# A two-layer Perceiver kernel on one Trainium2 core: its RWKV stage issued in three pieces a block

## The chip, the core and the metric

The kernel runs on one core of one Trainium2 chip. The core has five engines that run at the same time, each through an instruction list of its own: PE (TensorE, matrix products and transposes; its weight loads are listed as PEld), DVE (VectorE, elementwise work, scans and reductions), ACT (ScalarE, functions such as exp), POOL (GpSimd, elementwise work) and SP (SyncE, which here issues most DMAs). An instruction that needs another engine's result waits on a semaphore, and everything behind it on its own engine waits with it. So the order in which an engine's list is written decides as much as the amount of work.

The metric is the device time of one execution in microseconds (us). The profile is one more execution, recorded by the hardware profiler.

## What is computed

The input x has 64 sequences of 32 tokens of width 256, 2048 tokens; the context has 64 sequences of 257 rows. Two layers of three residual parts each run one after the other:

```python
x = x + _L0_xattn_ref(_layernorm(x), ctx_1024, ctx_1024, mask, ...)   # cross attention
x = x + _L0_attn_ref(_layernorm(x), ...)                              # RWKV
x = x + _L0_ffn_ref(_layernorm(x), ...)                               # 8 experts, top 2
x = x + _L1_xattn_ref(_layernorm(x), ctx_1024, ...)                   # quantized cross attention
x = x + _L1_attn_ref(_layernorm(x), ...)                              # state-space recurrence
x = x + _L1_ffn_ref(_layernorm(x), ...)                               # experts, top 1
```

The part that the change touches is the RWKV, whose two halves are a time mix (a recurrence over the 32 tokens of a sequence) and a channel mix:

```python
h = layernorm(x, ln1_g, ln1_b)
hh = time_shift(h)                     # the token before, 0 for the first
xk = h * tm_k + hh * (1 - tm_k)        # likewise xv, xr
k, v = xk @ Wk.T, xv @ Wv.T
sr = sigmoid(xr @ Wr.T)
x = x + (sr * wkv(time_decay, time_first, k, v)) @ Wo.T     # wkv: the recurrence
h = layernorm(x, ln2_g, ln2_b)
hh = time_shift(h)
xk = h * cm_k + hh * (1 - cm_k)        # likewise xr
kk = square(relu(xk @ Wck))
return x + sigmoid(xr @ Wcr.T) * (kk @ Wcv)
```

All of it works within a sequence, so blocks of whole sequences are independent of each other.

## The kernel before

The tokens are cut into 4 blocks of 512, and a block into 4 tiles of 128 tokens (4 sequences each). The residual stream x stays in on-chip memory for the whole kernel, one buffer a block (`k.x[b]`); every stage adds to it in place. All matrix products are in f32.

There are six stages, each a function that sets up its weights and returns what runs one block:

- `_stage0`, the first cross attention (here "stage 0"): `s0(b)` is a head (norm, transposes, query) and four tiles, 16 in all. A tile computes scores (L259), a softmax, the weighted sum (L292), the output product and its addition to x (L300). It also quantizes the context for the fourth stage: GpSimd multiplies the loaded context cT by its scales (L248), VectorE rounds, and a DMA stores the result (cq). `steps()` closes this.
- `_stage1`, the RWKV: `s1(b)`, L487 to L548, described below.
- `_stage2`, the first expert layer: `s2(b)` normalizes, computes the router's logits (L585), a softmax and the choice of two (L595 to L616) on VectorE, transposes the gates (gT, L619), then for each tile adds the gated bias (beps, L626) and the products of all 8 experts (weps, L631), which VectorE scales and adds to x (L633).
- `_stage3`, the second cross attention: `s3(lo, hi)` runs some of its 32 units (eight a block): scores L881, softmax, transposes (pt, L907), weighted sum (L915) and, with `last`, the closing norms and products of the block; the last of them is named vl_ps.
- `_stage4`, the state-space recurrence: `ahead(b)`, `gates(b)`, `recur(b)`; a block's recurrence is 32 groups of a multiply g on GpSimd (L1096), exponentials on ScalarE (L1100), scans on VectorE (L1101), a multiply hc (L1102) and a sum on GpSimd (L1107).
- `_stage5`, the second expert layer: up (L1250) and acc (L1258) products.

**One block of the RWKV.** VectorE takes the moments of the four tiles and an inverse root is made in twelve small GpSimd steps (`_rsqrt`, L90 to L93). `norm_to` (L435) writes the normalized rows hn (L446), PE transposes them (tps, L124), and ScalarE copies them into `hT`, a padded buffer in which channels lie on the partitions and tokens along the row. `shift_mix` (L408) takes the difference of `hT` and its shifted self and makes the mixes from it. Then `recur(c, ...)` (L449) runs once for each half c of the 256 channels: projections k, v and r (L432), a scan for the running maximum (L460), exponentials, two more scans (bb L474, aa L475), a reciprocal (L481), and the product with the gate sr (L484 on GpSimd, rw L485 on VectorE). GpSimd makes e2bv (L466) and v (L478) between. After both halves the output projection (wo, L507) is added to the normalized rows xn, which GpSimd made at L502, and to x. A second norm, transposes and shift mix follow, then the gate product (cr, L520) with a sigmoid, and the channel mix: eight groups of up products (ck, L528), Relu (L530) on ScalarE, square (kk, L531) on GpSimd and four products into the sum (cv, L540), with `up` two groups ahead; at the end VectorE multiplies by the gate (sg, L545) and GpSimd adds to x (L546).

**Buffers.** The recurrence's temporaries come from the pool `u1` with 9 buffers; each half needs six of them (v, sr, pp, e1, aa, bb). The padded buffers kp, e1b, e2b, e2bv exist once for each half; `hT` exists once and serves both norms of a block. hn, xn and sg share three buffers (tag "rows"), the mixes three others (tag "mix").

**Order.** The program is written stage by stage in `layers` (L1284 on). The framework that the kernel is written in schedules each engine's list when the kernel is built, ahead of the run: instructions whose inputs are expected ready are taken by the place at which they were emitted. So the order in `layers` is the priority, and an instruction that was emitted earlier goes first where both are ready. The lists are fixed after that. In the order of before, `s1(0)` is emitted behind `s0(1)`, `s1(1)` behind `s0(2)`; `s1(2)` and `s1(3)` are emitted at the end of their group, behind `s0(3)`, `s2(0)` and the first eight units `s3(0, 8)`, so that they fill what these leave free. The pools of the RWKV lie on the left side of the memory and are released when `s1(3)` is done; the state-space stage's buffers come there.

Of the kernel before, what the change touches and what calls it, by code (L numbers as in the profile page):

```python
# [8 lines left out]
F32 = mybir.dt.float32  # L9
# [6 lines left out]
P = 128  # L16
NB, T, S, D = 64, 32, 257, 256
NTOK = NB * T
NT = NTOK // P
NBLK = 4  # L20
# [336 lines left out]
def _stage1(k, pool):  # L357
# [4 lines left out]
    nc, i = k.nc, k.i  # L362
    w, u, wk, sm1 = pool("w1", 1), pool("u1", 9), pool("wk1", 1), pool("small1", 2)
    pa, pb = pool("psa1", 2, space=bass.MemoryType.PSUM), pool("psb1", 2, space=bass.MemoryType.PSUM)
# [13 lines left out]
    def padded(name, fill, shape=(16, T + 1)):  # L378
        t = w.tile([P, *shape], F32, name=name, tag=name)
        nc.gpsimd.memset(t, fill)  # L380
        return t

    wt, kp, e1b, e2b, e2bv = [], [], [], [], []
    for c in range(2):
        wt.append(padded(f"wt{c}", BIG))
        nc.vector.tensor_copy(wt[c][:, :, 1:], wdec[:, c : c + 1].unsqueeze(2).to_broadcast([P, 16, T]))
        kp.append(padded(f"kp{c}", BIG))
        e1b.append(padded(f"e1b{c}", 0.0))
        e2b.append(padded(f"e2b{c}", 0.0))
        e2bv.append(padded(f"e2bv{c}", 0.0))  # L390
    hT = padded("hT", 0.0, (2, 16, T + 1))

# [12 lines left out]
    def rows(name):  # L405
        return wk.tile([P, 4, D], F32, name=name, tag="rows", bufs=3)

    def shift_mix(names):  # L408


        def mix(name):
            return wk.tile([P, 2, 16, T], F32, name=name, tag="mix", bufs=3)

# [20 lines left out]

    def norm_to(xs, mean, scale, g, b):  # L435

# [49 lines left out]

    def block(b):  # L487
        x = k.x[b]
# [5 lines left out]
        _rsqrt(k, r8, [(mv[:, :, 1], 1.0, LN_EPS), (mv[:, :, 1], 1.0 + LN_EPS, LN_EPS * LN_EPS)], "1", sm1)  # L494
        norm_to(x, mv[:, :, 0:1], r8[:, 4:8], "L0_attn_ln1_g", "L0_attn_ln1_b")
        xk, xv, xr = shift_mix(["L0_attn_tm_k", "L0_attn_tm_v", "L0_attn_tm_r"])
        rw = wk.tile([P, 2, BT], F32, name="rw", tag="rw", bufs=1)
        for c in range(2):
            recur(c, xk, xv, xr, rw)
        xn = rows("xn")  # L500
        for j in range(4):
# [9 lines left out]

        mv2, rstd2 = _stats(k, [xn[:, j, :] for j in range(4)], "1b", sm1)
        norm_to(xn, mv2[:, :, 0:1], rstd2, "L0_attn_ln2_g", "L0_attn_ln2_b")
        xk, xr = shift_mix(["L0_attn_cm_k", "L0_attn_cm_r"])
        sg = rows("sg")
        for j in range(0, 4, 2):
            p = pa.tile([P, 2, D], F32, name="cr", tag="a")
            for f in range(2):
                for c in range(2):
                    nc.tensor.matmul(p[:, f, :], xr[:, c, (j + f) * P : (j + f + 1) * P], wT["cr"][:, c, :], start=c == 0, stop=c == 1)  # L520
            nc.scalar.activation(sg[:, j : j + 2, :], p, AF.Sigmoid)

        cvs = [pb.tile([P, 2, D], F32, name="cv", tag="b") for _ in range(2)]
# [23 lines left out]

    return block  # L548

# [729 lines left out]
def layers(k, out):  # L1279
# [13 lines left out]
    with left0:  # L1293
        s1 = _stage1(k, opened(left0, "left"))
        with ExitStack() as es:
            s0, steps = _stage0(k, opened(es, "right"))
            s0(0)
            for b in range(1, NBLK):
                s0(b)
                if b < NBLK - 1:  # L1300
                    s1(b - 1)
            steps()
# [7 lines left out]
        s3(0, 8, first=True, last=True)  # L1310
        s1(NBLK - 2)
        s1(NBLK - 1)
    with right, right3, left:
        pool = opened(left, "left")
# [130 lines left out]
```

## Time and profile before

| | us |
|---|---|
| median of three runs | 2054.96 |
| the runs | 2054.96, 2054.93, 2056.96 |
| the profiled execution, its own time | 2053.01 |
| its span, from the first to the last instruction | 2051.2 |

| engine | busy us | share of the span | instructions |
|---|---|---|---|
| PE | 1618.9 | 79% | 6323 |
| PE weight loads | 819.6 | 40% | 6323 |
| DVE | 1367.5 | 67% | 2475 |
| ACT | 983.5 | 48% | 2142 |
| POOL | 1062.7 | 52% | 1189 |

| mark in the span | us |
|---|---|
| channel mix of block 0 on PE | 219 to 247 |
| recurrence of block 1 (first scan to last rw) | 275.8 to 312.8 |
| channel mix of block 1 on PE | 349 to 377 |
| last sum of stage 0 | 396.6 |
| recurrence of block 2 | 401.1 to 438.6 |
| first matmul of the first expert layer (beps, L626) | 440.5 |
| first scores of the second attention (L881) | 484.0 |
| end of that attention's first block (vl_ps) | 690.9 |
| RWKV of block 3 ends (its last x, L546) | 705.5 |
| first scan of the state-space stage (L1101) | 778.1 |
| end | 2051.2 |

How to read what follows. A profile line of the timeline begins with the start in us and the length, then the engine, the source line, the operation, its output and inputs by the program's names, tile shapes (rows by columns for PE, partitions by elements otherwise), and how many equal instructions in a row it stands for. Where a bracket ends it, it holds the idle time of the engine just before and what ended it: `[11.47 <-PE cv L540]` is 11.47 us without work until PE's cv of L540 was done. Lines of the kernel are named L531 and so on. No engine is full over the span: the shares are means over stages with different limits, and the granted clock of PE, 0.831 of full speed on average, differs from stage to stage.

### The profile page before, as it was taken

Reading aid. Unit: us, or ns where it says so; the run is one execution under the profiler, and the core shown is the slowest. Engines: PE = TensorE matmul, PEld = TensorE weight load, DVE = VectorE, ACT = ScalarE, POOL = GpSimd, SP = SyncE. Lnnn points to the kernel's source line nnn. Section 1 sums busy time; section 2 is a strip of 40 time slices with the busy share of each in tenths; the row PEclk is TensorE's granted clock in tenths of the full one; section 3 lists DMA queues with packets and bytes.
Section 4 is the critical chain, followed back from the end, with each engine's and each line's share of the span. In section 5 each row is a group of like instructions: output and inputs, shape, how many; then the busy total and the mean of one; then the engine's idle time right before and its main releaser. Section 6 shows DMA issues by size and latency. Waiting matters only on the chain. (4 is left out here: it accounts for less than half of the span.)

```text
span 2051.2 us, 20219 instructions
## 1 busy us (share of the span) xinstructions
PE 1618.9 (79%) x6323; PEld 819.6 (40%) x6323; DVE 1367.5 (67%) x2475; ACT 983.5 (48%) x2142; POOL 1062.7 (52%) x1189
## 2 busy tenths in 40 slices
PE   4775967759979888765788969878879677688898
PEld 3332524425645543433443434444434233233343
DVE  4488487575475459989965887864778785886200
ACT  2454343313455254444427656637567454564332
POOL 5344656423142306776641776771477766998000
PEclk9677867879989998556689779988789889899999
DMA  6754324210000211222101222302123211442121
GB/s 223 234 188 135 113 72 145 64 41 21 21 21 2 61 28 42 58 56 61 42 32 48 73 66 89 92 21 69 52 62 89 54 52 58 107 118 63 51 82 41
DMA packets 88379, 151.26 MB, mean 74 GB/s; under 512 B 7740, under 2 KB 52300, under 8 KB 86224
## 3 DMA queue, kind: packets, MB, share of 16 engines
q1 hardware_dynamic: 85428, 148.75, 24.1%
q10 hardware_dynamic: 2844, 1.22, 0.2%
q8 instruction: 50, 0.82, 0.2%
q14 instruction: 57, 0.47, 0.1%
HBM read 139.03 MB, written 10.92 MB: 73 GB/s over the span
## 5 line engine op out<-in xcount | busy, mean ns | idle before, releaser
L1096 POOL TENSOR_TENSOR g<-dtx,bc 128x1024 f32<-128x1024 f32 x128 | 301.5, 2359 | 155.8 <-DVE h L1101 79.6
L1101 DVE TENSOR_TENSOR_SCAN h<-h,g 128x512 f32<-128x512 f32 x256 | 306.7, 1218 | 55.2 <-ACT h L1100 47.3
L1107 POOL TENSOR_TENSOR xc<-xc,hc 128x1024 f32<-128x1024 f32 x128 | 302.7, 2368 | 32.0 <-DVE hc L1102 22.8
L1250 PE MATMUL up<-xT,w 128*128 128x512 f32 x512 | 286.4, 675 | 34.5 <-ACT hid L1252 32.7
L1258 PE MATMUL acc<-hid,w 128*128 128x512 f32 x512 | 269.1, 647 | 21.1 <-ACT hid L1254 21.1
L1100 ACT ACTIVATE h<-dt,A 128x512 f32<-128x512 f32 x256 | 172.3, 691 | 155.5 <-DVE hc L1102 155.1
L892 ACT ACTIVATE p<-sc,nm 128x256 f32<-128x256 f32 x256 | 117.7, 471 | 135.8 <-DVE nm L888 121.9
L881 PE MATMUL sc<-kT,qm 32*128 32x256 f32 x512 | 147.3, 496 | 31.9 <-DVE od L921 21.9
L1102 DVE TENSOR_TENSOR hc<-h,bc 128x512 f32<-128x512 f32 x256 | 169.0, 677 | 1.6
L1250 PEld LDWEIGHTS up<-xT,w 128*128 128x128 f32 x512 | 98.2, 209 | 158.6 <-issue 84.0
L631 PE MATMUL weps<-we,xT 128*128 128x512 f32 x256 | 149.4, 710 | 14.1 <-DVE x L627 7.7
L1258 PEld LDWEIGHTS acc<-hid,w 128*128 128x128 f32 x512 | 100.1, 206 | 140.6 <-issue 100.9
L1252 ACT ACTIVATE hid<-up,chan 128x512 f32<-128x512 f32 x128 | 87.2, 681 | 133.4 <-PE up L1250 133.4
L90 POOL TENSOR_TENSOR rs_t<-rs_r 128x4 f32<-128x4 f32 (+4 forms) x168 | 37.3, 225 | 190.4 <-DVE rs_r L88 178.9
L881 PEld LDWEIGHTS sc<-kT,qm 32*128 32x128 f32 x512 | 86.2, 230 | 84.4 <-DVE od L921 32.9
L907 PE MATMUL pt_ps<-ident,p 128*128 128x128 f32 x512 | 94.3, 317 | 23.7 <-ACT p L892 16.4
L886 DVE TENSOR_REDUCE nm<-sc 128x2 f32<-128x512 f32 x128 | 86.2, 684 | 39.0 <-PE sc L881 38.3
L909 ACT COPY pt<-pt_ps 128x512 f32<-128x512 f32 x128 | 74.2, 586 | 58.1 <-PE pt_ps L907 57.8
L907 PEld LDWEIGHTS pt_ps<-ident,p 128*128 128x128 f32 x512 | 65.5, 159 | 79.3 <-ACT p L892 36.9
L1272 DVE SCALAR_TENSOR_TENSOR last<-rT,gt,x 128x256 f32<-128x256 f32 x16 | 7.6, 478 | 125.4 <-PE rT L1271 125.4
L531 POOL TENSOR_TENSOR kk<-kk 128x512 f32<-128x512 f32 x32 | 34.1, 1072 | 110.1 <-ACT kk L530 107.2
L915 PE MATMUL oT_ps<-pt,v 128*32 128x128 f32 x1024 | 74.5, 313 | 18.2 <-ACT pt L909 18.1
(404 smaller groups left out, 3182.5 us busy)
## 6 DMA issues: line engine op xcount, KB each, us to landing
bc<-rows SPq DMA_DIRECT2D x64, 512.0 KB
w<-in_L_ffn_w_dram SPq DMA_DIRECT2D x64, 512.0 KB
cT<-in_ctxT_dram SPq DMA_DIRECT2D x16, 1028.0 KB
cq<-cq SPq DMA_DIRECT2D x32, 514.0 KB
cn<-in_ctx_dram SPq DMA_DIRECT2D x64, 256.0 KB
scb<-scales SPq DMA_DIRECT2D x16, 514.0 KB
kb<-steps SPq DMA_DIRECT2D x16, 514.0 KB
x<-in_x_dram SPq DMA_DIRECT2D x4, 512.0 KB
```

The source lines that it names most:

```text
L631: nc.tensor.matmul(ps, xT[:, c, r], we[:, c, e : e + 2, :], start=c == 0, stop=c == 1)
L881: nc.tensor.matmul(sc[h][:, f, :], qm[r, e + f].rearrange("p l n g -> p (l n g)"), kTs[e][r, f, :], start=True, stop=True,)
L892: nc.scalar.activation(w_[:, f, h - h0, :], sc[h][:, f, :], AF.Exp, bias=nm[:, e + f, h : h + 1], accum_out=sm[:, e + f, h : h + 1],)
L907: nc.tensor.transpose(pt_ps[:, h, m, :], ws[e, hp][:, f, h, m * P : (m + 1) * P], k.ident)
L1096: nc.gpsimd.tensor_tensor(g, dtx[:, c2 : c2 + 2], bc[:, 0:1, :].to_broadcast([P, 2, BT]), ALU.mult)
L1100: nc.scalar.activation(h, dt, AF.Exp, scale=A[:, c2 + c, n : n + 1])
L1101: nc.vector.tensor_tensor_scan(h, h, g[:, c, :], 0.0, ALU.mult, ALU.add)
L1102: nc.vector.tensor_tensor(hc[:, c, :], h, bc[:, 1, :], ALU.mult)
L1107: nc.gpsimd.tensor_tensor(y[:, c2 : c2 + 2], y[:, c2 : c2 + 2], hc, ALU.add)
L1250: nc.tensor.matmul(u, w1[e][:, c, q * P : (q + 1) * P], xT[:, c, :], start=c == 0, stop=c == 1)
L1252: nc.scalar.activation(hid[e][:, q, :], u, AF.Identity, bias=b1)
L1258: nc.tensor.matmul(acc[o], w2[e][:, q, o * P : (o + 1) * P], hid[e][:, q, :], start=n == H, stop=n == E * H + H - 1)
```

## The change

The RWKV of a block is cut into three pieces that can be emitted apart. `time_mix(b)` goes up to the recurrence and returns its moments and rw; `between(b)` has the output projection, the second norm, its shift mix and the gate product with its sigmoid, and returns the mixed rows xk and the gate sg; `channel_mix(b)` has the eight groups of ck, Relu, square and cv, and the addition to x. The arithmetic is the same.

A new `s1(b)` emits `time_mix(b)`, then `channel_mix(b - 1)`, then `between(b)`. It is called behind each of `s0(1)`, `s0(2)` and `s0(3)`, for blocks 0, 1 and 2. So block 2 is now emitted ahead of `steps()`, `s2(0)` and the first eight units of the second attention. What was emitted behind these as blocks 2 and 3 is now block 3 (with the channel mix of block 2 in it) and the channel mix of block 3.

A channel mix now lives beside the next time mix, so the buffers change: there are two padded `hT` of which one serves the first norms and one the second; hn, xn, sg and the mixes share six buffers under one tag in place of two tags with three each; the pool `u1` has 8 buffers in place of 9; and the two halves share one e2bv buffer.

```diff
-    w, u, wk, sm1 = pool("w1", 1), pool("u1", 9), pool("wk1", 1), pool("small1", 2)
+    w, u, wk, sm1 = pool("w1", 1), pool("u1", 8), pool("wk1", 1), pool("small1", 2)
...
-        e2bv.append(padded(f"e2bv{c}", 0.0))
-    hT = padded("hT", 0.0, (2, 16, T + 1))
+        e2bv.append(e2bv[0] if c else padded("e2bv", 0.0))
+
+    hTs = [padded(f"hT{n}", 0.0, (2, 16, T + 1)) for n in range(2)]
...
-        return wk.tile([P, 4, D], F32, name=name, tag="rows", bufs=3)
-
-    def shift_mix(names):
+        return wk.tile([P, 4, D], F32, name=name, tag="rows", bufs=6)
+
+    def shift_mix(hT, names):
...
-            return wk.tile([P, 2, 16, T], F32, name=name, tag="mix", bufs=3)
+            return wk.tile([P, 2, 16, T], F32, name=name, tag="rows", bufs=6)
...
-    def norm_to(xs, mean, scale, g, b):
+    def norm_to(hT, xs, mean, scale, g, b):
...
-    def block(b):
+    def time_mix(b):
...
-        norm_to(x, mv[:, :, 0:1], r8[:, 4:8], "L0_attn_ln1_g", "L0_attn_ln1_b")
-        xk, xv, xr = shift_mix(["L0_attn_tm_k", "L0_attn_tm_v", "L0_attn_tm_r"])
+        norm_to(hTs[0], x, mv[:, :, 0:1], r8[:, 4:8], "L0_attn_ln1_g", "L0_attn_ln1_b")
+        xk, xv, xr = shift_mix(hTs[0], ["L0_attn_tm_k", "L0_attn_tm_v", "L0_attn_tm_r"])
         rw = wk.tile([P, 2, BT], F32, name="rw", tag="rw", bufs=1)
         for c in range(2):
             recur(c, xk, xv, xr, rw)
+        return mv, r8, rw
+
+    def between(b, mv, r8, rw):
+
+        x = k.x[b]
+        xs = [x[:, j, :] for j in range(4)]
         xn = rows("xn")
...
-        norm_to(xn, mv2[:, :, 0:1], rstd2, "L0_attn_ln2_g", "L0_attn_ln2_b")
-        xk, xr = shift_mix(["L0_attn_cm_k", "L0_attn_cm_r"])
+        norm_to(hTs[1], xn, mv2[:, :, 0:1], rstd2, "L0_attn_ln2_g", "L0_attn_ln2_b")
+        xk, xr = shift_mix(hTs[1], ["L0_attn_cm_k", "L0_attn_cm_r"])
...
             nc.scalar.activation(sg[:, j : j + 2, :], p, AF.Sigmoid)
+        return xk, sg
+
+    def channel_mix(b, xk, sg):
+        x = k.x[b]
...
-    return block
+    return time_mix, between, channel_mix
...
-        s1 = _stage1(k, opened(left0, "left"))
+        time_mix, between, channel_mix = _stage1(k, opened(left0, "left"))
         with ExitStack() as es:
             s0, steps = _stage0(k, opened(es, "right"))
+
+            c = {}
+
+            def s1(b):
+                t = time_mix(b)
+                if b:
+                    channel_mix(b - 1, *c[b - 1])
+                c[b] = between(b, *t)
+
             s0(0)
             for b in range(1, NBLK):
                 s0(b)
-                if b < NBLK - 1:
-                    s1(b - 1)
+                s1(b - 1)
             steps()
...
         s2(0)
         s3(0, 8, first=True, last=True)
-        s1(NBLK - 2)
         s1(NBLK - 1)
+        channel_mix(NBLK - 1, *c[NBLK - 1])
```

## The prediction

> **What bounds the kernel now.** I read the chain that ended last first. It runs back from the end only to 1568 us and is made of the state-space recurrence and the last expert layer, so the RWKV stage isn't on the part that is shown; what the stage decides is when that later work starts. The built order of the changed program agrees with the old one from the second half of the first state-space recurrence on (after its 16th of 128 multiplies g, GpSimd's counts of earlier work are equal in both), so I carry any shift there to the end unchanged. The question is when the first scan of L1101 runs; it is at 778.1 us now. I then cut the stretch before it at the events that the change moves: busy time of each engine by window (columns: window, length, busy us and instructions of PE, weight loads, DVE, ACT, POOL, then granted clock, DMA share, GB/s).
>
> ```profile
> 219.00:247.00 28.00, 27.72 (x98) 18.03 (x97) 8.62 (x13) 8.75 (x21) 18.11 (x14) 1.00 0.30 98
> 247.00:349.00 102.00, 66.48 (x312) 36.33 (x311) 84.54 (x127) 45.14 (x127) 57.65 (x60) 0.70 0.35 114
> 349.00:377.00 28.00, 28.00 (x99) 18.23 (x97) 2.51 (x3) 5.02 (x10) 11.94 (x17) 1.00 0.06 20
> ...
> 397.00:440.00 43.00, 17.02 (x56) 8.90 (x54) 39.23 (x86) 14.24 (x21) 18.84 (x38) 0.67 0.31 94
> 440.00:484.00 44.00, 41.20 (x126) 19.50 (x126) 27.70 (x84) 3.58 (x9) 8.57 (x30) 0.94 0.00 0
> 484.00:550.00 66.00, 65.89 (x341) 42.82 (x340) 28.43 (x74) 33.06 (x100) 17.50 (x20) 0.92 0.10 33
> 550.00:600.00 50.00, 42.65 (x217) 22.70 (x216) 39.30 (x71) 29.80 (x73) 15.11 (x18) 0.92 0.00 1
> 600.00:650.00 50.00, 41.84 (x189) 25.25 (x189) 30.64 (x85) 20.89 (x57) 14.16 (x41) 0.80 0.07 22
> 650.00:691.00 41.00, 41.00 (x263) 24.37 (x263) 14.35 (x37) 20.07 (x55) 10.29 (x20) 1.00 0.18 54
> ```
>
> 219 to 247 and 349 to 377 are the channel mixes of blocks 0 and 1: PE is full and DVE nearly empty. Between them, and from 397 to 440, DVE is full (84.5 of 102, 39.2 of 43) and PE starves. From 484 to 691 PE is the bound: 191.4 us busy of 207. The timelines of DVE and PE show the handovers:
>
> ```profile
> 223.63 1.08 DVE L446 TENSOR_SCALAR hn<-x,mv,r 128x256 f32<-128x256 f32 x3
> 246.22 0.69 DVE L545 TENSOR_TENSOR sg<-cv,sg 128x512 f32<-128x512 f32 x1 [11.47 <-PE cv L540]
> 250.81 0.66 PE L124 MATMUL tps<-ident,hn 128*128 128x128 f32 x4
> 275.77 1.25 DVE L460 TENSOR_TENSOR_SCAN pp<-wt,kp 128x528 f32<-128x528 f32 x1
> 296.83 2.07 PE L507 MATMUL wo<-w_L_attn_WoT,rw 128*128 128x256 f32 x4 [9.57 <-DVE rw L485]
> 312.12 0.69 DVE L485 TENSOR_TENSOR rw<-aa,sr 128x512 f32<-128x512 f32 x1 [1.07 <-POOL sr L484]
> 326.00 5.54 DVE L446 TENSOR_SCALAR hn<-xn,mv,rstd 128x256 f32<-128x256 f32 x4 [2.03 <-POOL rstd L93]
> 343.02 5.45 PE L520 MATMUL cr<-w_L_attn_WcrT,d 128*128 128x256 f32 x16
> 376.55 0.69 DVE L545 TENSOR_TENSOR sg<-cv,sg 128x512 f32<-128x512 f32 x1 [21.10 <-PE cv L540]
> 396.22 0.42 DVE L300 TENSOR_TENSOR x<-o_ps,x 128x256 f32<-128x256 f32 x1 [0.66 <-PE o_ps L298]
> 436.77 1.02 PE L619 MATMUL gT_ps<-ident,pr 128*8 128x128 f32 x4 [12.27 <-DVE pr L616]
> ```
>
> Block 1's normalized rows are ready at 224.7, but their transposes stand behind block 0's channel mix on PE and run at 250.8. Its recurrence takes 275.8 to 312.8, 37 us; block 2's took 401.1 to 438.6, the same. 396.6 is the end of stage 0.
>
> **The change, part by part.** No engine gets work or loses it, and no DMA is issued by the moved pieces; what moves is the order. On SP the loads of stage 0 and the weights of the later stages keep their number, and the stage-3 loads come after the last cq store as before.
>
> 1. Block 1's transposes go in front of block 0's channel mix: 250.8 to 224.7, 26 us earlier. The recurrence then starts at 275.8 - 26 = 250.
>
> 2. The channel mix of block 0 (28 us of PE) lies beside that recurrence. The order on GpSimd chains the two: two squares (L531, 1.04 us) and then the two matrix groups of 1.72 us stand behind the recurrence's last sr multiply (L484). Hence 250 + 37 + 2.1 + 3.4 = 292.5; the output projection, now in one piece, about 4.5 (16 passes between 0.22 and 0.38 us), ends at 297, against 313.56 + 3.96 = 317.5.
>
> 3. From there to the end of cr takes 31 us now (317.5 to 348.5); I keep it: 328. Behind it stand attention tiles 14 and 15 (two matrix chains of some 5 and 8 us by the rows at 336 to 343) and tile 16, which took 19.4 us from its scores at 377.2 to its sum at 396.6 with no channel mix in it. Stage 0 ends at 328 + 5 + 8 + 16 to 20 = 357 to 361; I take 357, 39 us earlier. Of the 39, 28 are the second channel mix, which is now emitted behind the end of stage 0 and must be paid there.
>
> 4. Block 2's recurrence starts with tile 16, about 346, and ends at 383 by the 37 us. Squares and groups as in step 2, with a reciprocal root of twelve GpSimd steps of 0.28 between them: 5.5 + 3.4, then 4.5 for the output projection: 396. Then cr: block 2's took 19 us from its last projection (471) to its start (490); 19 and 4 more: 419. Only behind cr do the expert router's logits (L585) stand now; they were at 414 to 416 before. 2 us for them, then 13: twelve DVE steps of the softmax (4.5 us by their rows) with block 3's shift mix (5.6) and an exponential between, and 1.6 for gT. The first expert matmul (L626) comes at 435, against 440.5. So most of the 39 us is spent here, on the channel mix and cr.
>
> 5. From L626 to the first scores L881 is 43.5 us now, PE 41 of 44 busy; block 3's projections come in (nine of twelve, 0.86 each, four of them in the way): 47. First scores at 482, against 484.0.
>
> 6. From the first scores to the end of the first attention (690.9) PE is the bound. It has done ahead of it 16 passes of cr, the transposes and nine projections, 13 us; but the new order puts in front of the end the last 12 products of block 3's channel mix (5.3) and 16 expert products (13.8), which stood behind it. Work 191.4 - 13 + 19 = 197. The idle 15.5 us of 550 to 650 (block 3's recurrence and its cr, waiting) get channel mix 2 and 3 as cover; I leave 6. The clock there was 0.80 and 0.92 where PE had gaps; full clock would shrink 84.5 us by some 11, I take 5. 482 + 197 + 6 - 5 = 680, 11 us earlier.
>
> 7. Behind it, the tail to the first scan was 690.9 to 778.1. The expert products that delayed the transposes of the next layer (715.9 to 724.4) and two products sg are gone from its way: 5 us, bounded by 0 and 8.5. The smaller pools (u 8 instead of 9, one e2bv) cost nothing: in every block the second half's scan already comes after the first half's reciprocal (286.3, 289.6), when slots are free, and e2bv's second write follows the first half's scan of it; the 37 us hide it, and without that cover it is one wait of about 2 us a block.
>
> Sum: 11 + 5 = 16 us. The profiled execution took 2053.0 us (span 2051.2), so 2037; the runs' median is 2 us higher, so 2054.96 - 16 = 2039; I say 2038.
>
> **A rule against the row.** The four hn of 326.00 took 5.54 us, those of 198.09 took 1.38; beside the slow ones GpSimd's cT multiply runs (325.92, 4.51 us). The Trainium skill, "SBUF — State Buffer", section "Who interferes with whom", says that VectorE and GpSimd lock a port pair against each other for a whole instruction. By that rule this change is dangerous, since it lays 16 squares beside two recurrences; an estimate from the rows is 16 x 1.04 = 17 us, and the gain would be gone. By the rows, the recurrence's 37 us hold such a collision already (rw at 291.79 took 4.98), so I add nothing.
>
> **Rivals.**
> A, the forecast, 0.50: 2038, own range 2026 to 2050.
> B, 0.16: the recurrences get faster when no attention operations stand between. Their DVE operations sum to 13 us a half by the rows (three scans 1.25, one reciprocal 3.34, eleven others 0.4 to 0.75), 26 a block against 37; with 28, two blocks give 18, and the other 6 us of the clock and 2 of the tail make 26: 2012. Against it: four recurrences in four surroundings took 37 to 46.
> C, 0.14: all is spent in front of the logits and in the tail: steps 6 and 7 give 3: about 2052.
> D, slower, 0.20: stage 0 doesn't end earlier. DVE is the bound there: between 219 and 397 it is busy 112 us, and steps 1 to 4 add some 8 in less time; collisions with GpSimd, whose cT multiply also holds back sr, stretch it. If the end stays at 396, step 4's 78 us, 47, 203 and the tail follow: 724 at the end of the first attention, 33 later, less 5: 2083. It decides from a stage 0 that ends after some 373.
> That the change doesn't take place is excluded: the built order shows it.
>
> **How the numbers follow.** A run can tell about 0.2%, 4 us, from none. Faster: A, B and a little of nothing else, 0.66. Same: 0.10 of C. Slower: D and the rest of C, 0.24. The range 2010 to 2062 cuts B's and D's outer parts, together 0.2.
>
> **What would show it.** In the changed profile: the first transposes hn of block 1 near 225 (step 1), PE waiting for GpSimd's kk within the channel mix (2), the last L300 near 357 (3), the first L626 near 435 (4), the first L881 near 482 (5), the eighth unit's last vl_ps near 680 (6), the first scan L1101 near 762 (7). Later rows must be shifted as a whole; if the distance from the first scan to the end changes by over 5 us, the assumption of equal later work is wrong. A stage 0 that ends after 373, or an L626 after 455, makes the prediction wrong.

## The result and the profile after

The changed kernel takes 2071.07 us (median of 8 runs, 2058.23 to 2079.91); the kernel before took 2053.82 us in the same comparison (8 runs, 2049.33 to 2058.81). The ratio is 1.0088, 95% interval 1.0070 to 1.0105: the change makes the kernel slower, by 17 us between the medians, where 16 us of gain were forecast.

The profiled execution took 2078.3 us (span 2076.5), 7 us above the median; a second profile of the same kernel (2078.9) shows the same marks within 3 us, and within 1.5 us from the end of stage 0 on. The steps below are measured in the first of the two, so they add up to 25 us in the span, of which the medians show 17. Line numbers behind the RWKV's first lines have moved: hn is L447, projections L433, scan L461, wo L514, cr L527, ck L539, square L542, cv L551, first scores L892, gT L630, beps L637, weps L642.

The engines' busy times first, from the page:

```profile
PE 1629.4 (78%) x6323; PEld 823.8 (40%) x6323; DVE 1386.5 (67%) x2475; ACT 982.7 (47%) x2141; POOL 1072.0 (52%) x1189
```

The instruction counts are those of before (ScalarE's but for one); VectorE is busy 19 us longer (1367.5 before), PE 10.5 and GpSimd 9.3. Whether that is the loss is a question for the experiments.

The windows of the changed kernel, cut at the same events as before (window, length, busy us and instructions of PE, weight loads, DVE, ACT, POOL, granted clock, DMA share, GB/s):

```profile
223.00:255.00 32.00, 27.85 (x134) 14.21 (x133) 28.70 (x30) 21.64 (x58) 20.17 (x10) 0.96 0.63 199
255.00:297.00 42.00, 33.50 (x111) 22.11 (x111) 24.82 (x32) 11.54 (x26) 21.90 (x26) 0.92 0.04 13
297.00:327.00 30.00, 20.14 (x103) 9.53 (x101) 21.75 (x49) 9.02 (x25) 12.49 (x29) 0.72 0.35 106
327.00:374.00 47.00, 33.91 (x131) 15.56 (x131) 35.18 (x48) 22.10 (x56) 29.29 (x23) 0.73 0.37 120
374.00:411.00 37.00, 31.79 (x95) 20.29 (x94) 26.30 (x37) 8.60 (x14) 21.18 (x24) 0.88 0.15 50
411.00:451.00 40.00, 21.34 (x86) 15.12 (x84) 26.65 (x81) 9.00 (x13) 20.97 (x38) 0.70 0.17 53
451.00:494.00 43.00, 40.47 (x114) 17.61 (x112) 31.78 (x77) 8.82 (x16) 5.86 (x14) 0.97 0.00 1
494.00:709.00 215.00, 201.57 (x1030) 119.09 (x1027) 108.95 (x271) 93.27 (x269) 56.98 (x114) 0.89 0.09 30
```

255 to 297 is block 0's channel mix beside block 1's recurrence: both PE and DVE now work there, where before each had such a stretch to itself. 374 to 411 is block 1's channel mix beside block 2's recurrence, and it stands behind stage 0 and ahead of the router. The last row is the first eight units of the second attention: 215 us, 8 longer than before, with 10 us more work on PE.

PE's timeline of the changed kernel, around the first of these:

```profile
221.99 1.55 PE L124 MATMUL tps<-ident,hn 128*128 128x128 f32 x6 [0.22 <-DVE hn L447]
254.23 0.62 PE L259 MATMUL sc<-cT,qk 128*32 128x257 f32 x2
254.78 5.42 PE L539 MATMUL ck<-mix,w_L_attn_WckT 128*128 128x512 f32 x12
279.30 3.78 PE L551 MATMUL cv<-w_L_attn_WcvT,kk 128*128 128x256 f32 x8 [7.09 <-POOL kk L542]
293.66 3.72 PE L514 MATMUL wo<-w_L_attn_WoT,rw 128*128 128x256 f32 x16
297.31 1.97 PE L259 MATMUL sc<-cT,qk 128*32 128x257 f32 x30
```

The transposes run at 222, as step 1 had it. PE waits 7.09 us within the channel mix for a square, and the output projection ends at 297.4 (297 forecast). GpSimd's timeline shows that the square stands behind the product v, which ended at 277.6, and ahead of the recurrence's last product sr; step 2 had it behind sr:

```profile
276.45 1.17 POOL L479 TENSOR_TENSOR v<-pp,v 128x512 f32<-128x512 f32 x1
277.74 3.50 POOL L542 TENSOR_TENSOR kk<-kk 128x512 f32<-128x512 f32 x3
281.69 1.17 POOL L485 TENSOR_TENSOR sr<-sr,bb 128x512 f32<-128x512 f32 x1 [0.45 <-DVE bb L482]
```

Two of the 32 score products of tile 12 (counted from 0) run at 254.2 and the other 30 at 297.3: these stand in PE's list behind the whole channel mix. Before, they ran at 283.6, in PE's idle time beside the recurrence.

The marks of the two kernels and of the forecast, read from the timelines:

| mark, us | before | forecast | after |
|---|---|---|---|
| recurrence of block 1 | 275.8 to 312.8 | 250 to 287 | 241.7 to 283.6 |
| wo of block 1 ends | 317.5 | 297 | 297.4 |
| cr of block 1 ends | 348.5 | 328 | 327.1 |
| stage 0 ends | 396.6 | 357 | 373.8 |
| recurrence of block 2 | 401.1 to 438.6 | 346 to 383 | 354.5 to 399.6 |
| first beps | 439.9 | 435 | 451.5 |
| first scores | 484 | 482 | 494 |
| eighth unit's last vl_ps | 691 | 680 | 709 |
| RWKV's last x | 705.4 | – | 670.9 |
| first scan of the state-space stage | 778.1 | 762 | 791.7 |
| end of the span | 2051.2 | 2035 | 2076.5 |

Up to the end of cr of block 1 the forecast holds within a few us, but for a recurrence that starts 8 us early. Then stage 0 ends 17 us late, and block 2's recurrence too; 17 us more are lost in the attention, and 12 behind the first scan.

### The profile page after: what moved, and what is told of

Read it like the earlier page. It is cut to its first block, busy times and chain, and to the rows that moved or that the text cites. A ratio compares the mean times of both kernels' runs of the same rounds, so it can differ in the third digit from the quotient of the medians.

```text
span 2076.5 us, 20230 instructions
## 1 busy us (share of the span) xinstructions
PE 1629.4 (78%) x6323; PEld 823.8 (40%) x6323; DVE 1386.5 (67%) x2475; ACT 982.7 (47%) x2141; POOL 1072.0 (52%) x1189
## 5 line engine op out<-in xcount | busy, mean ns | idle before, releaser
L892 PE MATMUL sc<-kT,qm 32*128 32x256 f32 x512 | 146.3, 488 | 28.3 <-DVE od L932 22.0
L642 PE MATMUL weps<-we,xT 128*128 128x512 f32 x256 | 140.2, 669 | 6.3 <-DVE x L638 4.1
L892 PEld LDWEIGHTS sc<-kT,qm 32*128 32x128 f32 x512 | 85.7, 227 | 84.6 <-DVE od L932 34.2
L248 POOL TENSOR_TENSOR cT<-cT,scb 128x2056 f32<-128x2056 f32 x16 | 73.8, 4613 | 43.7 <-DMA scb<-scales 24.8
```

Of the source, the lines that this page charges most:

```text
L642: nc.tensor.matmul(ps, xT[:, c, r], we[:, c, e : e + 2, :], start=c == 0, stop=c == 1)
L892: nc.tensor.matmul(sc[h][:, f, :], qm[r, e + f].rearrange("p l n g -> p (l n g)"), kTs[e][r, f, :], start=True, stop=True,)
```

## The experiments

The main theory: the split is good; the loss is made by block 2's pieces and block 1's channel mix standing ahead of the router, and by a different order of the later stages that comes with it. The edits are shown shortened, with the block numbers written out.

**1. The split alone.** Block 2 goes back behind the first eight units.

```diff
                 s0(b)
-                s1(b - 1)
+                if b < NBLK - 1:
+                    s1(b - 1)
...
         s3(0, 8, first=True, last=True)
+        s1(NBLK - 2)
         s1(NBLK - 1)
         channel_mix(NBLK - 1, *c[NBLK - 1])
```

> The three pieces and the new buffers stay, block 2 goes back to its old place behind the first eight units of the second attention (the channel mix of block 1 goes there with it). Main theory, the loss is made by the work of block 2 that stands in front of the router and by the later order that follows from it: stage 0 ends at 374 as in the changed kernel, the first beps (L626 of before) comes at about 412 in place of 451, the first scores at about 455, the first scan of the state-space stage at 745 to 760, and the time is 2020 to 2040, faster than before by 15 to 30 us. Rival 1, the split itself is the loss, since the channel mix beside the recurrence holds up the last four attention tiles of stage 0: beps not before 440 and a time of 2053 to 2075. Rival 2, the smaller buffers stall the recurrences: like the main theory, but 5 to 13 us are missing from the gain.

Measured: 2035.97 us (6 runs), ratio to the kernel before 0.9910 (0.9887 to 0.9933): 20 us faster than before, 35 faster than the changed kernel. Stage 0 ends at 370.1, beps comes at 415.5, the first scan at 756.0. The main theory holds; the split is not the loss.

**2. The earlier block alone.** The kernel before with whole blocks, block 2 called behind `s0(3)`.

```diff
                 s0(b)
-                if b < NBLK - 1:
-                    s1(b - 1)
+                s1(b - 1)
...
-        s1(NBLK - 2)
         s1(NBLK - 1)
```

> The kernel before, with whole blocks and the old buffers; only block 2 is called behind the last tiles of stage 0 and so ahead of the router and the first eight units. Main theory: stage 0 ends at 396 as before, the router and the first scores wait for block 2, scores at 520 to 540 in place of 484, of which the second attention gives back some 33 us that it no longer has to do; first scan 790 to 800, time 2065 to 2080, slower. Rival 1 (the split is the loss): within 5 us of before, 2050 to 2058. Rival 2 (buffers): the same as rival 1.

Measured: 2076.36 us (6 runs), ratio 1.0098 (1.0071 to 1.0125). The first scores come at 529, as expected, but the attention gives nothing back (33 us were expected): 207.1 us for its eight units, and the first scan only at 813.7, 14 us behind its range. So the earlier block by itself costs 20 us, about as much as the split gains. The two don't add up to the change: with the split in place the same move costs 35 us (2035.97 to 2071.07), since the channel mix of block 1 then goes ahead of the router with it.

**3. The buffers alone.** The lists of all engines are those of before, by the traces too.

```diff
-    w, u, wk, sm1 = pool("w1", 1), pool("u1", 9), pool("wk1", 1), pool("small1", 2)
+    w, u, wk, sm1 = pool("w1", 1), pool("u1", 8), pool("wk1", 1), pool("small1", 2)
...
-        e2bv.append(padded(f"e2bv{c}", 0.0))
+        e2bv.append(e2bv[0] if c else padded("e2bv", 0.0))
```

> The kernel before with 8 buffers in place of 9 for the recurrence's temporaries and with one e2bv buffer for both halves; the order of every engine is that of before. Main theory and rival 1: no difference, 2050 to 2058, the recurrences of blocks 1 and 2 take 37 us each. Rival 2 (the buffers stall the recurrence): these take 42 to 45 us and the time is 2060 to 2070.

Measured: 2055.23 us (12 runs), ratio 0.9991 (0.9974 to 1.0007); block 1's recurrence takes 37.0 us. These two smaller buffers cost nothing in that order; the shared tag and the second `hT` were not tried in it.

**4 and 5. Which piece ahead of the router costs.** In 4 only the time mix of block 2 stays ahead, in 5 its piece between too; what is taken away goes behind the router (4) or, the channel mix of block 1, behind the attention (5).

```diff
+            t2 = time_mix(2)
             steps()
...
         s2(0)
+        channel_mix(1, *c[1])
+        c[2] = between(2, *t2)
         s3(0, 8, first=True, last=True)
```

> The changed kernel, but only the time mix of block 2 is emitted ahead of the router; the channel mix of block 1 and the piece between (output projection, second norm, gate product) of block 2 are emitted behind the first router block, ahead of the second attention. The order behind the first scan is that of the changed kernel. Main theory: beps at about 415 in place of 451, first scores at about 462 in place of 494, the attention longer by the 8 us of wo and cr, first scan 770 to 778, and a time of 2050 to 2060, 12 to 20 us under the changed kernel. Rival 1 (the split is the loss): no gain over the changed kernel, 2066 to 2076.

```diff
+            t2 = time_mix(2)
+            c[2] = between(2, *t2)
             steps()
...
         s3(0, 8, first=True, last=True)
+        channel_mix(1, *c[1])
```

> The changed kernel, but the channel mix of block 1 goes behind the first eight units of the second attention; the time mix of block 2 and its piece between stay ahead of the router. Main theory, the 28 us of the channel mix that PE does ahead of the router are most of the price: first beps at 416 to 425 (451 in the changed kernel, 418 where the piece between was taken away too), first scan 768 to 780, time 2045 to 2060. Rival 3, the price is the wait for the recurrence of block 2, with its output projection and second norm on DVE and GpSimd: beps not before 438, time 2062 to 2075.

Measured: experiment 4 takes 2048.52 us (12 runs), ratio 0.9964 (0.9946 to 0.9982), with beps at 417.8 and the first scan at 766.6; scan and time lie a little under their ranges. Experiment 5 has beps at 427.2, 2 us above its range, and takes 2066.37 us (4 runs), ratio 1.0060 (1.0041 to 1.0080), 6 us above its range, with the first scan at 776.7.

The first beps comes at 415.5 in experiment 1, at 417.8 with the time mix of block 2 emitted ahead of the router, at 427.2 with the piece between too, and at 451.5 in the changed kernel, with the channel mix of block 1 as well. But PE does this channel mix ahead of the first beps in 1 and 4 too (82 of its 96 matmul records in 1, all of them in 4), as fill. PE's timelines show the difference, experiment 4 first, the changed kernel below:

```profile
376.89 6.03 PE L539 MATMUL ck<-mix,w_L_attn_WckT 128*128 128x512 f32 x12
409.67 1.85 PE L596 MATMUL lg<-w_L_ffn_Wg,xT 128*128 128x8 f32 x16
416.81 1.03 PE L551 MATMUL cv<-w_L_attn_WcvT,kk 128*128 128x256 f32 x4
417.77 0.69 PE L637 MATMUL beps<-be,both 8*128 8x256 f32 x2
```
```profile
373.62 6.38 PE L539 MATMUL ck<-mix,w_L_attn_WckT 128*128 128x512 f32 x12
411.32 3.72 PE L514 MATMUL wo<-w_L_attn_WoT,rw 128*128 128x256 f32 x16
432.15 6.18 PE L527 MATMUL cr<-w_L_attn_WcrT,d 128*128 128x256 f32 x16 [5.32 <-DVE d L426]
438.17 1.85 PE L596 MATMUL lg<-w_L_ffn_Wg,xT 128*128 128x8 f32 x16
```

In 4 the router's logits (lg) stand within the channel mix, and its end runs while VectorE makes the gates. In the changed kernel they stand behind the whole channel mix, the output projection, the second norm and cr. So the channel mix by itself costs little there; what costs is the chain in front of the logits: 9 us with the piece between (5 against 4), and 24 more with the channel mix in front of that piece.

The attention of experiment 5 takes only 198 us and ends at 665, 8 us ahead of experiment 1, and yet its first scan is 21 us later. Something else holds it.

**6 and 7. What holds the first scan.** In 6 the channel mix of block 0 goes behind the last tiles of stage 0; in 7 only block 0 of the RWKV is emitted ahead of the router. Both start from experiment 1.

```diff
             s0(2)
             t1 = time_mix(1)
-            channel_mix(0, *c[0])
             c[1] = between(1, *t1)
             s0(3)
+            channel_mix(0, *c[0])
             steps()
```

> As the first experiment (block 2 in its old place), but the channel mix of block 0 is emitted behind the last tiles of stage 0 and behind the piece between of block 1. Theory on step 3, stage 0's tail is late because tile 12 (counted from 0) stands on PE behind the channel mix of block 0 and the output projection of block 1: stage 0 ends at 350 to 360 in place of 370, but the channel mix now lies ahead of the router, so that beps comes at 400 to 415 in place of 415.5; time 2020 to 2036. Rival 4, the tail of stage 0 goes at the pace of its loads and of VectorE, whatever stands on PE: it ends at 365 to 375, and with 28 us of channel mix behind it beps comes at 425 to 435; time 2045 to 2055.

```diff
             s0(2)
-            t1 = time_mix(1)
             channel_mix(0, *c[0])
-            c[1] = between(1, *t1)
             s0(3)
             steps()
...
         s3(0, 8, first=True, last=True)
+        t1 = time_mix(1)
+        c[1] = between(1, *t1)
```

> As the first experiment, but only block 0 of the RWKV (all three pieces) is emitted ahead of the router; blocks 1 to 3 stand behind the first eight units. If everything that isn't needed for the first scan is a loss ahead of the router, stage 0 ends at 340 to 355 and beps comes at 380 to 395. If the second attention is bound by PE's whole work, as step 6 had it, it then takes 225 to 250 us for its eight units in place of 216, and the first scan comes at 745 to 765; the later order is that of the changed kernel, which costs 10 to 14 us: 2035 to 2055. If the fill work lies in gaps, the eight units take 207 to 216: first scan 720 to 735, time 2005 to 2030.

Measured: in 6 stage 0 ends at 334, 36 us earlier than in experiment 1 and below the range, so its tail was indeed held by what stood on PE and the other engines ahead of its tiles. PE's timeline of experiment 6 shows tile 12 running between the halves of the output projection, as before the change:

```profile
267.86 2.07 PE L514 MATMUL wo<-w_L_attn_WoT,rw 128*128 128x256 f32 x4 [8.78 <-DVE rw L486]
283.28 2.07 PE L298 MATMUL o_ps<-w_L_xattn_WvT,avT 128*128 128x256 f32 x4 [0.46 <-ACT avT L294]
```

beps comes at 400.4 and the attention ends at 672, 18 us ahead of the kernel before; still the time is 2053.78 us (10 runs), ratio 0.9995 (0.9978 to 1.0012), far above the expected one. In 7 beps comes at 375.3 and the attention ends at 643.6, 47 us ahead, and the time is 2064.02 us (5 runs), ratio 1.0051 (1.0030 to 1.0072); the attention took 225 us, but the first scan came at 778.4, later than either expectation. VectorE's timeline of experiment 7 shows the first reason:

```profile
673.84 0.23 DVE L88 TENSOR_SCALAR rs_r<-rs_r 128x4 int32<-128x4 int32 x2
702.71 0.69 DVE L556 TENSOR_TENSOR sg<-cv,sg 128x512 f32<-128x512 f32 x1 [28.64 <-PE cv L551]
705.28 2.22 DVE L116 TENSOR_SCALAR xn<-x,mv,rstd 128x256 f32<-128x256 f32 x3
```

The norms of the state-space stage (xn, L116) stand in VectorE's list behind the last product of block 3's channel mix (sg), and VectorE waits 28.64 us for that channel mix on PE. PE's timeline of experiment 5 shows the second:

```profile
700.70 7.13 PE L642 MATMUL weps<-we,xT 128*128 128x512 f32 x16
708.98 7.13 PE L642 MATMUL weps<-we,xT 128*128 128x512 f32 x16
717.89 1.12 PE L1025 MATMUL inps<-xT,w_L_attn_in_projT 128*128 128x512 f32 x2
```

The products of the first expert layer for block 1 (weps) were emitted ahead of the state-space stage and stand in PE's list ahead of its first projection (inps). In 5 and 7 none of them ran within the attention's first block, so they run here. So the first scan has three gates: the attention's last addition to x in its first block, which follows 18 to 23 us behind that block's last vl_ps, the last product of the RWKV, and the expert products that are left. (Times in the table in us; "products" is PE's time on beps and weps between the later of the two columns before it and the first inps.)

| kernel | attention's first block ends | its last x | RWKV's last sg | products | first inps | first scan |
|---|---|---|---|---|---|---|
| before | 691 | 712 | 703 | 10 | 727 | 778 |
| after | 709 | 728 | 669 | 0 | 742 | 792 |
| 1, split alone | 673 | 695 | 675 | 5 | 708 | 756 |
| 2, early alone | 736 | 754 | 660 | 7 | 766 | 814 |
| 4 | 684 | 703 | 658 | 0 | 717 | 767 |
| 5 | 665 | 684 | 686 | 26 | 718 | 777 |
| 6 | 673 | 692 | 699 | 15 | 717 | 770 |
| 7 | 644 | 666 | 704 | 19 | 727 | 778 |

Where the attention's x is the later one, the first inps follows 12 to 17 us behind it, in ten of the thirteen profiles (those that the table leaves out too), the kernels before and after among them. In 6 and 7 the RWKV is the later one, and in 5 both come within 3 us and the products take the time. The first scan follows 46 to 59 us behind the first inps. So in the change the attention's end decides on both sides: the RWKV's last product came 34 us earlier, which brought nothing, and the attention's end 18 us later. That the buffers, which the state-space stage takes over from the RWKV, put the norms behind it and not the emission order alone, was not tried.

**8. The changed kernel again.**

> The changed kernel again, for a second profile. If the 15 us between the first scan of block 1 (L1101 of before, its 65th) and its last come from the later order, that stretch takes 231 to 237 us again (218 in the kernel before); if they were an accident of one execution, 216 to 222.

Measured: 233.2 us, and 2070.17 us (4 runs). So the stretch is no accident.

**9, 10 and 11. The later order, and the order of the early pieces.** All three start from experiment 1 with block 2 in its old place. 9 emits the channel mix of block 1 ahead of the time mix of block 2, behind the attention; 10 emits the channel mix of block 0 ahead of the time mix of block 1; 11 emits the channel mix of block 1 between the router block and the attention.

```diff
         s3(0, 8, first=True, last=True)
-        t2 = time_mix(2)
         channel_mix(1, *c[1])
+        t2 = time_mix(2)
```

> As the first experiment (block 2 behind the first eight units), but the channel mix of block 1 is emitted ahead of the time mix of block 2. PE's list then has that channel mix among the last attention tiles of stage 0, ahead of the router, and behind the first scan every engine's list is that of the changed kernel in place of that of the first experiment. Theory of the two gates (the first scan comes 78 to 87 us behind the last vl_ps of the eighth unit, or 69 to 79 us behind the RWKV's last x, whichever is later): stage 0 ends at 372 to 385, first scan 760 to 775. Theory of the later order: the stretch from the 65th to the 128th scan takes 231 to 237 us, and the time is 2045 to 2060. If that stretch is 216 to 222, the later order isn't what costs the 15 us.

```diff
             s0(2)
-            t1 = time_mix(1)
             channel_mix(0, *c[0])
+            t1 = time_mix(1)
             c[1] = between(1, *t1)
```

> As the first experiment, but the channel mix of block 0 is emitted ahead of the time mix of block 1 (behind the tiles of block 2 of stage 0). If the gain of the first experiment comes from the order of these two, the channel mix beside the recurrence, then stage 0 ends at 385 to 397 in place of 370 and most of the 20 us are gone: time 2046 to 2056. If it comes from the channel mix of block 1 no longer being ahead of the end of stage 0, then stage 0 ends at 365 to 375 here too and the time is 2030 to 2042.

```diff
         s2(0)
+        channel_mix(1, *c[1])
         s3(0, 8, first=True, last=True)
         t2 = time_mix(2)
-        channel_mix(1, *c[1])
```

> As the first experiment, but the channel mix of block 1 is emitted between the first router block and the second attention, ahead of the time mix of block 2, as in the experiment before the last; the list of PE is the same as there up to the first attention units, and behind the first scan it is that of the first experiment. Theory of the later order: the stretch from the 65th to the 128th scan takes 217 to 222 us, and the time is 10 to 14 us shorter than there for the same first scan: 2033 to 2048.

The expectation for 11 calls experiment 9 "the experiment before the last". Measured: 9 takes 2036.70 us (4 runs, ratio 0.9916, 0.9889 to 0.9943), less than expected, as stage 0 ends at 365.2 and its first scan comes at 754.7, both ahead of their ranges; 10 takes 2050.31 us (10 runs, 0.9981, 0.9966 to 0.9997); 11 takes 2030.53 us (4 runs, 0.9884, 0.9856 to 0.9913), the fastest and 2 us under its range.

10 answers neither way: stage 0 ends at 369.7 as in experiment 1, but block 1's recurrence runs at 275 to 314 as before, beps comes 7 us later than in experiment 1, and the RWKV ends at 703. It is 14 us slower than experiment 1, so most of the split's gain needs the channel mix beside the recurrence; some 4 us are left without it (0.9981).

On the later order: the windows from the 65th to the 128th scan (block 1's recurrence of the state-space stage), of the kernel before, of the changed one, of 9 and of 11:

```profile
1130.00:1348.00 218.00, 180.22 (x730) 87.01 (x730) 180.00 (x253) 136.40 (x291) 161.86 (x120) 0.81 0.26 78
```
```profile
1138.00:1371.00 233.00, 185.64 (x776) 89.48 (x775) 182.75 (x259) 143.82 (x309) 161.19 (x108) 0.82 0.24 73
```
```profile
1092.00:1329.00 237.00, 185.87 (x780) 90.12 (x783) 185.88 (x260) 144.50 (x310) 162.29 (x111) 0.82 0.24 72
```
```profile
1106.00:1327.00 221.00, 175.62 (x728) 85.21 (x729) 180.51 (x254) 136.48 (x291) 162.59 (x120) 0.84 0.29 77
```

But for experiment 2, which has one of its own, each kernel has one of two lists here: that of before (some 730 PE instructions in the stretch, also in 1, 3, 6, 10, 11: 218 to 221 us) or that of the changed kernel (some 780, with more of the attention's products between the scans, also in 4, 5, 7, 9: 232 to 237 us). Part of the loss is made up ahead of the stretch. From the first scan to the end of the span the first list takes 1273 to 1279 us and the second 1279 to 1290, on average 1276 and 1285, 9 us more. But the profiles of the changed kernel and of experiment 4 lie 7 to 9 us above their kernels' medians; with the medians in place of the profiled times, and the first scans as profiled, the averages are 1278 and 1281. And 9 and 11, which differ little ahead of the first scan, differ by 5 us behind it in the profiles and by 3 by the medians, where 10 to 14 were expected. So the second list costs some 3 to 9 us, and the size stays open. No kernel with the early part of the changed one and the later list of before was run, so the cost is shown on the other kernels, not by undoing it in this one.

For the best version, 11, the windows of stage 0's tail, of the router, of the way to the first scores and of the attention's first block:

```profile
298.00:365.00 67.00, 49.16 (x243) 25.28 (x236) 39.31 (x77) 23.34 (x71) 38.58 (x50) 0.80 0.36 111
365.00:399.00 34.00, 28.59 (x108) 17.81 (x106) 26.22 (x80) 8.19 (x14) 16.21 (x30) 0.90 0.52 158
399.00:455.00 56.00, 46.84 (x123) 20.96 (x122) 46.48 (x93) 13.01 (x24) 14.60 (x30) 0.88 0.00 0
455.00:664.00 209.00, 190.25 (x1030) 115.01 (x1029) 115.84 (x264) 102.84 (x282) 59.95 (x105) 0.92 0.08 26
```

Here nearly half of block 1's channel mix (46 of 96 matmul records) lies between the last attention tiles of stage 0, in place of block 2's projections, and stage 0 still ends at 365. The other half runs ahead of the logits, which end at 384: 34 us from stage 0's end to beps, in place of 78. The attention's first block ends at 664.

## Why the prediction was wrong

- **Step 1 held, step 2 as a sum.** The transposes came 26 us earlier, and wo ended at 297.4 (297 forecast). But two errors cancel in it. The recurrence took 42 us and not 37; it started 8 us ahead of the forecast and ended at 283.6, 3 ahead of it. From there to the last matrix group (293.7) it took 10 us and not 5.5: the last two squares (285.9 and 289.3) waited for ScalarE's Relu and not for sr.
- **Step 3 failed in its last term, the tail of stage 0.** cr ended at 327 (328 forecast), then the last three tiles took 47 us in place of 29. The step added 5, 8 and 16 us for them; they took 10, 9 and 28. The last one (345.8 to 373.8) has block 2's shift mix and first scans beside it. VectorE's timeline of the changed kernel:

```profile
345.76 4.39 DVE L426 SCALAR_TENSOR_TENSOR mix<-d,chan,hT 128x512 f32<-128x512 f32 x1
350.07 0.47 DVE L264 TENSOR_SCALAR s<-sc,qb 128x257 f32<-128x257 f32 x1
373.35 0.41 DVE L300 TENSOR_TENSOR x<-o_ps,x 128x256 f32<-128x256 f32 x1
```

  The mix of 0.73 us takes 4.39 beside GpSimd's cT multiply (345.07, 4.54 us), the tile's softmax waits behind it, and its last sum stands 6 us behind the recurrence's scans. In experiment 11, whose block 2 starts only at 395, the last tile takes 22 us. In experiment 6, where tile 12 moreover doesn't stand behind the channel mix and block 2's recurrence starts at 373, stage 0 ends at 334.
- **Step 4 failed in block 2's recurrence,** which it had from 346 to 383 and which ran from 354.5 to 399.6. From stage 0's end to beps it had 78 us and 77.7 were measured, but that is luck: the logits don't wait for stage 0's end, they stand behind cr (in the kernel before they ran at 410.4 to 412.2, not at 414 to 416). What the path hangs on is the end of the recurrence, and from there to beps 52 us were forecast and 51.9 measured. The recurrence came 8.5 us later and took 45 us and not the 37 that were carried over, though in the kernel before block 0's took 47. GpSimd's timeline of the changed kernel shows why:

```profile
358.01 4.55 POOL L248 TENSOR_TENSOR cT<-cT,scb 128x2056 f32<-128x2056 f32 x1
366.79 0.46 POOL L93 TENSOR_TENSOR cdq<-rs_r,rs_t 128x128 f32<-128x128 f32 x1
367.20 1.17 POOL L467 TENSOR_TENSOR e2bv<-e2b,v 128x512 f32<-128x512 f32 x1
```

  e2bv, which the scan needs, stands behind the last cT multiply and the inverse roots of `steps()` (355.8 to 367.2). The step moved block 2 past `steps()` without looking at GpSimd's list there. The price of the pieces that it moved ahead of the router was right: 34 us by the forecast (78 in place of 44 from stage 0's end to beps), 34.5 measured (77.7 in place of 43.2).
- **Step 5 was 4 us too long** (42.7 measured, 47 forecast).
- **Step 6 failed: 215 us in place of 198.** It took the stretch as bound by PE and its work as 197; PE was busy 201.6. Counting each of PE's rows until the next one starts, the attention's own products make 84 us of the stretch before and 86 after, the RWKV's 84 and 81, the expert layer's 24 and 34: the RWKV's part fell by only 3, since the rest of block 3's channel mix came in, and the expert layer's rose by 10 with products of block 1. Nothing within the stretch waits for these; but what isn't done of them here runs behind it, as in experiment 5, whose stretch has 3 us of the expert layer and takes 198. The 15.6 us of idle stayed at 13.4 (6 forecast), and the clock gave nothing: 0.91 before, 0.89 after (5 us forecast). So of the 17 us 5 are work, 7 idle time and 5 the clock.
- **Step 7 held:** 82.6 us from the attention's end to the first scan, 82 forecast and 87.2 before. The expert products between the attention's last x and the first inps fell from 10 us to 0, as it had it; they are paid in step 6. The prediction saw neither the RWKV's end as a gate nor the products as one; here they didn't bind, but they bound experiments 5, 6 and 7, where the attention ends 26, 18 and 47 us earlier than before and the first scan comes 1, 8 and 0 us earlier.
- **The carried shift failed by 12 us in the profile.** GpSimd's counts agree at the 16th and 17th multiply g, but not at the 33rd (716 and 727 instructions ahead of it), and by the traces the lists of PE, VectorE and GpSimd are the same only from 1372 to 1378 us of the kernel before on, behind block 1's recurrence. By the runs above the second list costs 3 to 9 of the 12 us.

In us, from the forecast's span of 2035.2 to 2076.5: 16.5 (step 4, up to beps), -4.3 (5), 16.9 (6), 0.6 (7), 11.6 (behind the first scan), in all 41.

**The rivals.** D, the slower one, had the right sign, but not the price: with a stage 0 that ends at 373.8 its terms put the attention's end at 702 and the time at some 2061, where 2071 was measured. Its mechanism, that VectorE and its collisions hold stage 0's end at 396, took place only in part, in the last tile; the split alone, with the same squares beside recurrences, is 20 us faster than before. C, that all is spent ahead of the router, is nearest to what happened: 39 us were to be won, 23 were, and 34 were put ahead of the router. B had nothing for it: no recurrence got shorter.

**The rule that was weighed.** The Trainium skill, "SBUF — State Buffer", section "Who interferes with whom", would have had the squares block VectorE for 17 us in all, by the estimate made from it. The changed kernel's VectorE is busy 19 us longer than before, but the split alone, which has the squares of block 0's channel mix beside a recurrence too, only 12 (1379.7), and 11, with 2030 us the fastest, less than before (1366.9). The collisions are there, as rows show (a product of the recurrence, L484, took 1.52 us beside a square and 0.68 without), but they did not decide the time.

## What to carry to other kernels

Find every gate of the stage that bounds the rest, here the end of the attention's first block, the end of the RWKV and the expert products that stand ahead in PE's list, and ask of each moved piece which gate it brings forward and which it pushes back. Work that is split off is worth most as fill where the engine idles (the last tiles of stage 0, or the time in which VectorE makes the router's gates), and is a loss where the one step that everything waits for (the router's logits) stands behind it in the list. A changed early order can change the scheduler's later lists as well, so equal counts at a few points do not make an equal order: compare the lists instruction by instruction on each engine, and also on GpSimd for what a moved step now stands behind.

## What the runs showed of the hardware that was not expected

In the changed kernel an instruction of VectorE waited for nearly the whole of a long GpSimd multiply: the one of L463 (L462 of before), with two inputs, takes 0.74 us, but took 4.87 beside the cT multiply that started 0.2 us ahead of it (242.69, 4.55 us). One with a single tensor input did so too: a norm hn (L447) took 4.63 us at 327.14, beside a cT multiply of 4.62 us that started at 326.99, and the two behind it 0.72 us together. It also went the other way: GpSimd's v took 5.31 us at 386.65, in place of 1.2 to 1.5, beside a chain of VectorE scans and products.

The changed kernel's runs lie further apart (2058 to 2080 us) than those of the kernel before (2049 to 2059), and its two profiled executions lie 7 and 9 us above the medians, at a like mean clock (0.827 and 0.826); the kernels with the same later list differ among themselves in this. Why, stays open.
